# The causal mask of self-attention: added by VectorE in PSUM, or by a matmul on TensorE

## The chip, the cores and the metric

One core of one Trainium2 chip runs the whole kernel. Time is in device microseconds from one launch; three runs of the kernel before gave 2084.55, 2084.80 and 2087.17 us, and their median, 2084.8 us, is the time before. Beside these stands one execution under the profiler, to which every line of a profile here belongs.

## The reference

A decoder layer on x of shape (4, 512, 512): self-attention with a causal mask (16 query heads in 4 groups, each group with one key and value head, head size 128), cross-attention, and a mixture of 8 experts with a shared one, each behind a layernorm. The part that the change touches:

```python
scale = 1.0 / jnp.sqrt(jnp.float32(D))
scores = jnp.einsum('bsgqd,btgd->bgqst', q, k) * scale
causal = jnp.tril(jnp.ones((s, s), dtype=bool))
scores = jnp.where(causal, scores, jnp.finfo(scores.dtype).min)
attn = jax.nn.softmax(scores, axis=-1)
out = jnp.einsum('bgqst,btgd->bsgqd', attn, v)
```

Each of the 512 queries of a sequence sees the keys up to its own place.

## The kernel before

Self-attention is the first stage, some 900 us of the whole. It loops over 4 sequences (b), 4 groups (g) and 4 query heads of a group (h), that is 64 heads. Matrices are in float32, and TensorE does a float32 matmul in two passes, so that the profile shows two instructions for each.

For one head:

- `project` (L232) makes the transposed queries qT, 128 x 512, from four matmuls of 512 columns into a PSUM tile pq, which ScalarE copies and scales (L248). Once a group it makes the keys kT in the same way.
- `softmax_rows` (L251) goes over the four blocks of 128 queries (i). Block i sees (i + 1) * 128 keys. One matmul (L258) writes the scores to the PSUM tile sc, of which there are two buffers. Only the last 128 columns, the diagonal block, need a mask: a second matmul (L265) adds it in PSUM, with the identity `ident16` as weights and `mask16` (0 on and below the diagonal, -3.0e38 above) as data, both in bfloat16. VectorE then takes the negated maximum of each row from PSUM (`nmx`, L268), and ScalarE computes the exponentials into pr, with nmx as bias and the sums as a second output (L271). When the four blocks are done, VectorE takes the reciprocals of the sums (L279) and scales pr (L282).
- `attend` (L285) transposes pr in blocks of 128 x 128 on TensorE (L290: 1, 2, 3 and 4 transposes for the four blocks, ten in all, into the PSUM tile tp), has them copied to prT (L294: by ScalarE for block 1, by VectorE for the others), and multiplies with the values (L297) into po, which ScalarE copies (L305).
- After the fourth head of a group, `add_projection` (L308) multiplies with the output weights into pj and adds to x on VectorE (L319). The last sequence's is left for the next stage.

The program text calls `attend` of a head after `softmax_rows` of the next one (`late`, from L332). Within this stage the order on each engine isn't that of the text: a planner of the framework orders the instructions by its own estimate of when each one's inputs and buffers are ready. So one finds, on TensorE, transposes of the head before and projections of the next head between the score matmuls. Dependencies, and the waits for them, the framework finds by itself. [...]

`make_causal_mask` writes the float32 mask `maskf`; two casts on VectorE (L61, L65) make `ident16` and `mask16` at the start. In the stages behind, the order is for the most part pinned to that of the text, and they don't use the mask.

Of the kernel before, what the change touches and what calls it, by code (L numbers as in the profile page):

```python
# [9 lines left out]
BF16 = mybir.dt.bfloat16  # L10
AF = mybir.ActivationFunctionType
ALU = mybir.AluOpType
# [3 lines left out]
P = 128  # L16
# [19 lines left out]
def decoder_kernel(  # L36
# [15 lines left out]
    nc = tc.nc  # L52
    const = ctx.enter_context(tc.tile_pool(name="const", bufs=1))
# [3 lines left out]

    ident = const.tile([P, P], F32, tag="ident", name="ident")
    make_identity(nc, ident)
    ident16 = const.tile([P, P], BF16, tag="ident16", name="ident16")  # L60
    nc.vector.tensor_copy(ident16, ident)  # L61
    maskf = const.tile([P, P], F32, tag="maskf", name="maskf")
    make_causal_mask(nc, maskf, mask_val=MASK)
    mask16 = const.tile([P, P], BF16, tag="mask16", name="mask16")
    nc.vector.tensor_copy(mask16, maskf)  # L65
    ones16 = const.tile([P, P], BF16, tag="ones16", name="ones16")
    nc.gpsimd.memset(ones16, 1.0)

# [110 lines left out]
    with ExitStack() as ph:  # L179
# [71 lines left out]
        def softmax_rows(b, g, h, qT, kT):  # L251
            pr = p2.tile([P, 10 * P], F32, tag="pr", name=f"pr{b}_{g}_{h}")
            nmx = small.tile([P, NT], F32, tag="nmx", name=f"nmx{b}_{g}_{h}")
            sm = small.tile([P, NT], F32, tag="sm", name=f"sm{b}_{g}_{h}")
            for i in range(NT):
                n = (i + 1) * P
                sc = ps.tile([P, S], F32, tag="sc", name=f"sc{b}_{g}_{h}_{i}")
                nc.tensor.matmul(  # L258
                    sc[:, :n],
                    lhsT=qT[:, i * P : n],  # L260
                    rhs=kT[:, :n],
                    start=True,
                    stop=False,
                )
                nc.tensor.matmul(  # L265
                    sc[:, i * P : n], lhsT=ident16, rhs=mask16, start=False, stop=True
                )
                nc.vector.tensor_reduce(  # L268
                    nmx[:, i : i + 1], sc[:, :n], AX.X, ALU.max, negate=True
                )  # L270
                nc.scalar.activation(  # L271
                    pr[:, OFF[i] : OFF[i] + n],
                    sc[:, :n],
                    AF.Exp,
                    bias=nmx[:, i : i + 1],
                    accum_out=sm[:, i : i + 1],
                )
            rs = small.tile([P, NT], F32, tag="rs", name=f"rs{b}_{g}_{h}")
            nc.vector.reciprocal(rs, sm)  # L279
            for i in range(NT):  # L280
                q = pr[:, OFF[i] : OFF[i] + (i + 1) * P]
                nc.vector.tensor_scalar(q, q, rs[:, i : i + 1], None, ALU.mult)  # L282
            return pr
# [48 lines left out]
        for b in range(B):  # L332
            xnT, v = norm_and_v(b)
            for g in range(NKV):
                kT = project(b, g, QPG, xnT)
                outs = []
                for h in range(QPG):
                    qT = project(b, g, h, xnT)
                    pr = softmax_rows(b, g, h, qT, kT)
                    if late is not None:  # L340
                        finish(*late)
                    late = (b, g, h, pr, v, outs)
# [137 lines left out]
    with ExitStack() as ph:  # L480
# [329 lines left out]
        for i in range(NU * 8 + LAG + 4):  # L810
            n, step = divmod(i, 8)
# [92 lines left out]
    with ExitStack() as ph:  # L904
# [8 lines left out]
        for d in range(1, TT):  # L913
            nc.tensor.matmul(
                pos[:, d:, :],
                lhsT=ones16,
                rhs=sel[:, : TT - d, :],
                start=False,
                stop=d == TT - 1,
            )  # L920
        tot = ps.tile([P, E], F32, tag="tot", name="tot")
        for d in range(TT):
            nc.tensor.matmul(
                tot, lhsT=ones16, rhs=sel[:, d, :], start=d == 0, stop=d == TT - 1
# [56 lines left out]
        for op, value in ((ALU.bitwise_and, P - 1), (ALU.arith_shift_right, 7)):  # L981
            i = p2.tile([P, TT2], I32, tag=f"i{value}", name=f"i{value}")
# [7 lines left out]
        for k in range(2):  # L990
# [37 lines left out]
            for d in range(TT):  # L1028
                nc.tensor.matmul(
                    pick,  # L1030
                    lhsT=at_place[:, d],
                    rhs=nums[:, d],
                    start=k == 0 and d == 0,
                    stop=k == 1 and d == TT - 1,
# [165 lines left out]
```

## Time and profile before

| what | value |
|---|---|
| time before, median of three runs | 2084.8 us |
| the profiled execution | 2085.54 us |
| its span, first to last instruction | 2083.8 us |
| mean granted clock of TensorE | 0.997 |
| self-attention's score matmuls, first to last | 37.3 to 898.9 us |
| TensorE busy, 235 to 450 us | 214.0 of 215 us |
| VectorE busy, 235 to 450 us | 80.9 of 215 us |
| ScalarE busy, 235 to 450 us | 59.6 of 215 us |
| one head without a group's extra work | 9.375 us |

A line of the page's first part gives, for each engine, its busy time, the share of the span and the number of instructions. A line of the groups of instructions gives the line of the kernel, the engine, the operation, the tile written and the tiles read, the shape of the operands, how often, then the total busy time and the mean time of one (ns), then how long the engine stood idle before such instructions and for whom. A line of the timeline gives the start, the duration, the engine, the line and the operation; x2 or x4 are so many like instructions in a row, taken together, and a bracket at the end gives the idle time before it and what ended it. A matmul's duration holds the latency until its result is written, so the durations of successive matmuls overlap: what each takes from TensorE is read from start to start. PEld is the loading of the weights, which runs beside the matmuls.

### The profile page before, as it was taken

Reading aid. Unit: us, or ns where it says so; the run is one execution under the profiler, and the core shown is the slowest. Engines: PE = TensorE matmul, PEld = TensorE weight load, DVE = VectorE, ACT = ScalarE, POOL = GpSimd, SP = SyncE. Lnnn points to the kernel's source line nnn. Section 1 sums busy time; section 2 is a strip of 40 time slices with the busy share of each in tenths; the row PEclk is TensorE's granted clock in tenths of the full one; section 3 lists DMA queues with packets and bytes.
Section 4 is the critical chain, followed back from the end, with each engine's and each line's share of the span. In section 5 each row is a group of like instructions: output and inputs, shape, how many; then the busy total and the mean of one; then the engine's idle time right before and its main releaser. Section 6 shows DMA issues by size and latency. Waiting matters only on the chain. (4 is left out here: it accounts for less than half of the span.)

```text
span 2083.8 us, 22685 instructions
## 1 busy us (share of the span) xinstructions
PE 2029.6 (97%) x8507; PEld 948.5 (46%) x8507; DVE 864.6 (41%) x1843; ACT 679.5 (33%) x1479; POOL 197.3 (9%) x182
## 2 busy tenths in 40 slices
PE   7999999999999999999999999999999999999996
PEld 4555555554555555542233333333333445555553
DVE  4433344442344334436666656566563351111111
ACT  2322332232223323323555454444444101111121
POOL 1000000000000000010202202020200011222222
PEclk9999999999999999999999999999999999999999
DMA  7000000000000000010003100100110255323321
GB/s 282 0 1 0 1 0 1 0 0 1 0 1 0 1 0 0 1 32 14 16 16 100 32 16 22 42 15 13 42 27 1 95 199 160 59 56 57 57 49 23
DMA packets 52509, 74.81 MB, mean 36 GB/s; under 512 B 9889, under 2 KB 27809, under 8 KB 52402
## 3 DMA queue, kind: packets, MB, share of 16 engines
q1 hardware_dynamic: 43666, 54.73, 8.5%
q0 software_dynamic: 8736, 18.62, 4.7%
q8 instruction: 70, 1.15, 0.2%
q14 instruction: 37, 0.30, 0.0%
HBM read 47.60 MB, written 18.61 MB: 32 GB/s over the span
## 5 line engine op out<-in xcount | busy, mean ns | idle before, releaser
L362 DVE TENSOR_REDUCE cnmx<-s 128x1 f32<-128x512 f32 x512 | 329.3, 685 | 199.3 <-PE s L362 199.2
L362 ACT ACTIVATE w<-s 128x512 f32<-128x512 f32 x512 | 277.9, 595 | 339.0 <-PE s L362 338.9
L362 PE MATMUL s<-ckT,cqT 32*128 32x512 f32 x1024 | 308.8, 640 | 1.0 <-DVE cnmx L362 1.0
L236 PE MATMUL pq<-xnT,wqk 128*128 128x512 f32 x640 | 300.9, 593 | 0.0
L362 PE MATMUL s<-cqT,ckT 32*128 32x512 f32 x1024 | 294.8, 640 | 0.0
L268 DVE TENSOR_REDUCE nmx<-sc 128x1 f32<-128x128 f32 (+3 forms) x256 | 125.8, 491 | 185.0 <-PE sc L265 184.8
L271 ACT ACTIVATE pr<-sc,nmx 128x128 f32<-128x128 f32 (+3 forms) x256 | 135.0, 527 | 156.0 <-DVE nmx L268 156.0
L294 DVE COPY prT<-tp 128x128 f32<-128x128 f32 (+2 forms) x192 | 97.0, 507 | 206.4 <-PE tp L290 206.3
L258 PE MATMUL sc<-kT,qT 128*128 128x128 f32 (+3 forms) x512 | 181.4, 463 | 0.0
L312 PE MATMUL pj<-wpr,oT 128*128 128x512 f32 x384 | 171.8, 596 | 0.0
L362 PE MATMUL sh<-fnT,sw 128*128 128x512 f32 x320 | 154.0, 613 | 0.0
L297 PE MATMUL po<-prT,v 128*128 128x512 f32 (+3 forms) x512 | 149.5, 434 | 4.3 <-DVE prT L294 4.3
L236 PEld LDWEIGHTS pq<-xnT,wqk 128*128 128x128 f32 x640 | 110.7, 191 | 85.5 <-issue 85.4
L362 PEld LDWEIGHTS s<-cqT,ckT 32*128 32x128 f32 x1024 | 80.7, 183 | 145.3 <-ACT w L362 108.6
L1112 DVE TENSOR_TENSOR hm<-h,sl 128x352 f32<-128x352 f32 x39 | 20.5, 525 | 284.6 <-PE h L1102 279.1
L362 PE MATMUL cpo<-w,vpad 128*32 128x512 f32 x1024 | 137.3, 608 | 0.0
L297 PEld LDWEIGHTS po<-prT,v 128*128 128x128 f32 x512 | 96.8, 190 | 84.3 <-issue 45.4
L1124 PE MATMUL y<-w3all,hT 128*128 (+1 forms) x234 | 109.8, 605 | 15.1 <-DVE hT L1120 15.1
L248 ACT ACTIVATE qT<-pq 128x512 f32<-128x512 f32 x64 | 38.2, 597 | 225.0 <-PE pq L236 225.0
L258 PEld LDWEIGHTS sc<-kT,qT 128*128 128x128 f32 x512 | 81.6, 189 | 56.1 <-ACT qT L248 20.2
L312 PEld LDWEIGHTS pj<-wpr,oT 128*128 128x128 f32 x384 | 69.5, 190 | 77.3 <-issue 71.0
L290 PE MATMUL tp<-ident,pr 128*128 128x128 f32 x640 | 102.3, 275 | 1.3 <-DVE prT L294 1.3
(162 smaller groups left out, 2000.6 us busy)
## 6 DMA issues: line engine op xcount, KB each, us to landing
w1all<-in_w1T SPq DMA_DIRECT2D x8, 704.0 KB
w2all<-in_w2T SPq DMA_DIRECT2D x8, 704.0 KB
wqk<-in_wqkvT SPq DMA_DIRECT2D x4, 1280.0 KB
x<-in_x SPq DMA_DIRECT2D x4, 1024.0 KB
wpr<-in_wprojT SPq DMA_DIRECT2D x4, 1024.0 KB
cqT<-cxnT SPq DMA_DIRECT2D x128, 32.0 KB
ckT<-ctxT SPq DMA_DIRECT2D x128, 32.0 KB
normed<-fxn SPq DMA_DIRECT2D x4, 1024.0 KB
```

The source lines that it names most:

```text
L236: nc.tensor.matmul(pq, lhsT=wqk[g][:, c, h * D : (h + 1) * D], rhs=xnT[:, c, :], start=c == 0, stop=c == NC - 1,)
L248: nc.scalar.mul(t, pq, QSCALE)
L258: nc.tensor.matmul(sc[:, :n], lhsT=qT[:, i * P : n], rhs=kT[:, :n], start=True, stop=False,)
L268: nc.vector.tensor_reduce(nmx[:, i : i + 1], sc[:, :n], AX.X, ALU.max, negate=True)
L271: nc.scalar.activation(pr[:, OFF[i] : OFF[i] + n], sc[:, :n], AF.Exp, bias=nmx[:, i : i + 1], accum_out=sm[:, i : i + 1],)
L290: nc.tensor.transpose(t[:, j, :], pr[:, OFF[i] + j * P : OFF[i] + (j + 1) * P], ident)
L294: copy(prT[:, : i + 1, i * P : (i + 1) * P], t[:, : i + 1, :])
L297: nc.tensor.matmul(po[:, j * P :], lhsT=v[j][:, g, :], rhs=prT[:, j, j * P :], start=j == 0, stop=j == NT - 1,)
L312: nc.tensor.matmul(pj, lhsT=outs[h][:, s * P : (s + 1) * P], rhs=wpr[g][:, h, :], start=h == 0, stop=h == QPG - 1,)
L362: i = getattr(self.engine, name)(*args, **kw)
L1112: nc.vector.tensor_tensor(hm, h2, sl, ALU.mult)
L1124: nc.tensor.matmul(y, lhsT=hT[:m, ic, :], rhs=w3all[:m, e, ic, :], start=ic == 0, stop=ic == len(IC) - 1,)
```

## The change

The second matmul goes. The diagonal block of sc is instead read from PSUM by VectorE, added to `maskf` and written back to the same place, ahead of the reduction. The two casts and the tiles `ident16` and `mask16` go as well. Nothing else is changed.

```diff
     ident = const.tile([P, P], F32, tag="ident", name="ident")
     make_identity(nc, ident)
-    ident16 = const.tile([P, P], BF16, tag="ident16", name="ident16")
-    nc.vector.tensor_copy(ident16, ident)
     maskf = const.tile([P, P], F32, tag="maskf", name="maskf")
     make_causal_mask(nc, maskf, mask_val=MASK)
-    mask16 = const.tile([P, P], BF16, tag="mask16", name="mask16")
-    nc.vector.tensor_copy(mask16, maskf)
...
                     lhsT=qT[:, i * P : n],
                     rhs=kT[:, :n],
                     start=True,
-                    stop=False,
-                )
-                nc.tensor.matmul(
-                    sc[:, i * P : n], lhsT=ident16, rhs=mask16, start=False, stop=True
+                    stop=True,
+                )
+                nc.vector.tensor_tensor(
+                    sc[:, i * P : n], sc[:, i * P : n], maskf, ALU.add
                 )
                 nc.vector.tensor_reduce(
                     nmx[:, i : i + 1], sc[:, :n], AX.X, ALU.max, negate=True
```

So in every block the reduction, and behind it the exponentials and the release of the buffer of sc, follow an instruction of VectorE instead of one of TensorE.

## The prediction

> **What bounds the kernel now.** I read the page first, then the groups of instructions by shape in the attention stage, then the timeline of one head on TensorE, VectorE and ScalarE, then the waits.
>
> ```profile
> PE 2029.6 (97%) x8507; PEld 948.5 (46%) x8507; DVE 864.6 (41%) x1843; ACT 679.5 (33%) x1479; POOL 197.3 (9%) x182
> ```
>
> TensorE sets the time, and VectorE is under half busy. From the groups by shape, two rows (busy us and mean ns after the bar):
>
> ```profile
> L265 PE MATMUL sc<-mask,ident 128*128 128x128 bf16 x256 | 56.1, 219 | 0.0
> ...
> L319 DVE TENSOR_TENSOR x<-pj,x 128x512 f32<-128x512 f32 x48 | 33.2, 691 | 111.5 <-PE pj L312 111.5
> ```
>
> The mask matmul's 219 ns is latency, not what it takes from TensorE. For that, read start to start on the TensorE timeline of one head, which recurs every 9.375 us (start, duration; x2 are the two passes of one float32 matmul, and the second start is not shown):
>
> ```profile
> 408.88 0.39 PE L258 MATMUL sc<-kT,qT 128*128 128x128 f32 x2
> 409.10 0.22 PE L265 MATMUL sc<-mask,ident 128*128 128x128 bf16 x1
> 409.16 0.65 PE L258 MATMUL sc<-kT,qT 128*128 128x256 f32 x2
> 409.64 0.22 PE L265 MATMUL sc<-mask,ident 128*128 128x128 bf16 x1
> 409.70 0.61 PE L290 MATMUL tp<-ident,pr 128*128 128x128 f32 x4
> 410.19 0.91 PE L258 MATMUL sc<-kT,qT 128*128 128x384 f32 x2
> 410.94 0.22 PE L265 MATMUL sc<-mask,ident 128*128 128x128 bf16 x1
> 411.00 1.10 PE L258 MATMUL sc<-kT,qT 128*128 128x512 f32 x2
> ```
>
> From 409.10 to 409.16: a mask costs TensorE 0.055 us. The transposes between row blocks 1 and 2 belong to the head before; they are cover. The chain through the other engines, first VectorE and then ScalarE:
>
> ```profile
> 404.36 0.18 DVE L279 RECIPROCAL rs<-sm 128x4 f32<-128x4 f32 x1 [0.25 <-ACT pr L271]
> 404.57 1.27 DVE L282 TENSOR_SCALAR pr<-pr,rs 128x128 f32<-128x128 f32 x4
> ...
> 409.36 0.29 DVE L268 TENSOR_REDUCE nmx<-sc 128x1 f32<-128x128 f32 x1 [1.06 <-PE sc L265]
> 409.90 0.43 DVE L268 TENSOR_REDUCE nmx<-sc 128x1 f32<-128x256 f32 x1 [0.25 <-PE sc L265]
> ```
>
> ```profile
> 409.68 0.37 ACT L271 ACTIVATE pr<-sc,nmx 128x128 f32<-128x128 f32 x1 [0.93 <-DVE nmx L268]
> ```
>
> The tile sc has two buffers, so row block 2's matmul needs the exponential of block 0, and block 3's that of block 1. Exponential 0 ends at 410.05, and the matmul starts 0.14 later, at 410.19. So TensorE already waits on this chain. The waits say it for block 3 (us in total, times, the longest), 0.25 us a head:
>
> ```profile
> PEld sc L258 <- ACT pr L271: 16.0, 63, 0.3
> ```
>
> The idle time of TensorE in a head: 0.06 behind mask 0 (the stream of a mask is too short to hide the next weight load); 0.16 at block 2 (the four transposes take 0.44, so they end at 410.14, and block 2, weights first, streams from 410.30, since its own 0.64 of streaming ends at 410.94); 0.085 at block 3 (it streams for 0.855 before 411.94, where its mask starts; hence from 411.085, against 411.00). Together 0.305.
>
> **What the Trainium skill says.** "TensorE: Matmul & The Clock Gate", back-to-back issue gap, gives N/2.4 + 2.5 ns, 56 ns for 128 columns; the trace has 0.055 us. "VectorE: DVE Perf Modes", the errata section, gives (N+151)/0.96 ns for a float32 tensor_tensor: 691 at 512, just what L319 shows, and 291 at 128. "Perfetto Trace Analysis", optimization strategy, says that a gap that repeats on the saturated engine "can mean there isn't enough SBUF/PSUM for the next tile"; the 0.25 us wait, 63 times, is that.
>
> **The change, part by part.** All sums are against the profiled execution, 2085.5 us (span 2083.8 and 1.7 around it); the median of the runs shown, 2084.8, is 0.7 lower.
>
> Removed, two casts at the start (0.20 and 0.22 us on VectorE): at most 0.2 us of the first layernorm. I take nothing: TensorE's first real matmuls, from 14.25, run beside weights that are still being loaded (the DMA engines are over 90% busy there), and these loads don't get earlier.
>
> Removed, 256 mask matmuls: 4 x 0.055 = 0.22 us a head, and the 0.06 idle behind mask 0. Blocks 0 and 1 are then through TensorE at 409.53 (two passes of 0.11 from 408.88, two of 0.213 from 409.10), 0.17 before 409.70.
>
> Added, 256 adds on VectorE, PSUM and SBUF in, PSUM out. No instruction of before writes PSUM from VectorE. The nearest row is L319 by the formula above, 0.29 us; the bounds are 0.27 and 0.35. The reduction reads what the add wrote: a dependent pair starts 0.03 after the first one's end (404.36 + 0.18, then 404.57). VectorE has the time: 4 x 0.29 on some 4.6 busy in 9.375.
>
> What this moves in the chain, first with TensorE's order as it is. Matmul 0's second pass starts at 408.99, lasts 0.28, and VectorE follows 0.04 later (as from the mask's end, 409.32, to 409.36): add 0 at 409.31 to 409.60, reduction 0 from 409.63 instead of 409.36. Everything behind it is 0.27 late: exponential 0 ends at 410.32, and block 2 streams from 410.57. Add 1 is queued behind reduction 0 (consecutive VectorE instructions overlap by 0.08): 409.84 to 410.13; reduction 1 to 410.58; exponential 1 from 410.61 to 411.08; block 3 may load at 411.22 and streams from 411.335, for 0.86, to 412.195. In the profile its mask is done at 412.00. So a head becomes 0.195 longer, although 0.22 of matmuls went. Behind that there is cover: adds 2 and 3 delay the copies to prT to some 414.0, where po was to start at 414.05; the scaling of L282 has 1.8 us of slack before its transposes.
>
> But TensorE's order is a planner's. It has put transposes of the head before, and projections, where the scores aren't ready: four transposes as shown, but in the first heads it was three and a projection:
>
> ```profile
> 52.69 0.50 PE L290 MATMUL tp<-ident,pr 128*128 128x128 f32 x3
> 53.02 1.02 PE L236 MATMUL pq<-xnT,wqk 128*128 128x512 f32 x2
> 53.88 0.81 PE L258 MATMUL sc<-kT,qT 128*128 128x384 f32 x2
> ```
>
> There block 2 doesn't wait (0.81 for its two passes, against 0.91). With a chain that is longer by 0.27 and two masks fewer ahead of the cover, 0.17 earlier, a planner that sees the add has about 0.4 more to fill: four more transposes at 0.11, but only three are left (three of a head's ten are done earlier, four are there). I take all seven. Each moved ahead of block 2 saves 0.11 behind block 3: 0.195 - 3 x 0.11 = -0.135 a head. Times 63 heads that have such cover: -8.5 us. The last head has nothing to cover it: its later add and copies cost some 0.45. Sum: -8, so 2077.5 profiled, or 2076.8 as a median.
>
> **The rivals**, as medians, the last head's 0.45 in each. *Full cover* (faster): the planner puts a projection (0.86 us) ahead of block 2, as in the early heads. All idle time goes with the masks: 0.22 + 0.305 = 0.525 a head, 33 us, 2052. For it: that the pattern exists; against: that the planner left it by the fourth head. A projection between blocks 2 and 3 alone lies between: with seven transposes, block 2 ends at 411.21, the projection at 412.07, block 3 at 412.93, against 413.19 before for the same work: -0.26, -16 us, 2069. I count it to the forecast's case.
>
> *Balance*: six transposes (-0.025 a head), or seven with an add of 0.35, which comes in twice in block 3's chain (-0.135 + 0.12): within 2 us of 2084.
>
> *The wait grows* (slower): four or five transposes stay ahead of block 2, because the planner prices the add below its real latency. The place is block 2's and 3's wait for the exponentials; the price 0.195 a head, 12 us, 2097 at four (0.315, 20 us, with an add of 0.35); it decides below six transposes, 0.195/0.11 = 1.8 above four. For it: that today's order already leaves 0.16 and 0.085 idle, so the planner is late by that much.
>
> *A worse order* (slower): the adds, waiting at the head of VectorE's queue for their matmul, hold back the copies to prT and with them po. Over 2100. Against it: 1.8 us of slack, and a VectorE half idle.
>
> **How the numbers follow.** Forecast 0.33; full cover 0.22; balance 0.10; the wait grows 0.25; a worse order 0.10. Change within 0.2% (4 us) is about what a measurement here can't tell from none. Faster 0.55, same 0.10, slower 0.35. The likeliest case's own range, from a projection ahead of block 3 to an add of 0.35, is 2069 to 2084. The range of 8 in 10 reaches from full cover to the growing wait with some of the dearer add: 2051 to 2100; it leaves out the worse order and the ends of the two neighbours.
>
> **What would show it.** On the timeline of a head: the number of transposes between blocks 1 and 2 (seven), block 2's start against exponential 0's end (0.14), the period (9.24; 9.57 if the wait grows, 8.85 with full cover). An add of 0.29 us and a reduction 0.03 behind it. The wait of block 3 for the exponential still there. Wrong if the add isn't within 0.27 to 0.35, if the order of TensorE is unchanged, or if another wait than the exponentials' ends last.

## The result, and the profile after

| | time before | time after | ratio, 95% interval |
|---|---|---|---|
| median of four runs each | 2085.94 us | 2070.34 us (2068.06 to 2070.88) | 0.9923 (0.9906 to 0.9941) |
| span of the profiled execution | 2083.8 us | 2066.2 us | |

The change makes the kernel 15.6 us faster, less than 1%. The forecast was 8. (The median before is of one run more than the 2084.8 us above.) In the changed kernel L254 is the score matmul, L261 the add, L264 the reduction, L267 the exponential, L286 the transposes, L293 po, L232 the projections. First the page's line of busy times, then the add's row among the groups of instructions (busy us and mean ns after the bar):

```profile
PE 2012.8 (97%) x8251; PEld 940.1 (45%) x8251; DVE 923.2 (45%) x2097; ACT 679.8 (33%) x1479; POOL 197.1 (10%) x182
...
L261 DVE TENSOR_TENSOR sc<-sc,maskf 128x128 f32<-128x128 f32 x256 | 75.3, 294 | 157.7 <-PE sc L254 157.7
```

TensorE has 256 instructions fewer and is still busy for 97% of the span, so it remains the bound. VectorE has 58.6 us more to do than its 864.6 before and is still under half busy: as a load the adds are no matter, only as links of a chain. The add takes 294 ns.

Next, one head of the changed kernel on TensorE's timeline:

```profile
105.20 0.82 PE L254 MATMUL sc<-kT,qT 128*128 128x128 f32 x4
105.85 0.93 PE L286 MATMUL tp<-ident,pr 128*128 128x128 f32 x7
106.79 0.91 PE L254 MATMUL sc<-kT,qT 128*128 128x384 f32 x2
107.54 1.02 PE L232 MATMUL pq<-xnT,wqk 128*128 128x512 f32 x2
108.40 1.02 PE L254 MATMUL sc<-kT,qT 128*128 128x512 f32 x2
109.26 2.32 PE L293 MATMUL po<-prT,v 128*128 128x512 f32 x8
...
114.32 0.82 PE L254 MATMUL sc<-kT,qT 128*128 128x128 f32 x4
```

Three things are new besides the missing masks. Seven transposes, not four, stand between blocks 1 and 2. A projection stands between blocks 2 and 3. And po follows block 3 at once, since no transposes are left to be done there. From 105.20 to 114.32 the head takes 9.12 us, where it was 9.375.

The chain through VectorE and ScalarE in the same head:

```profile
105.62 0.30 DVE L261 TENSOR_TENSOR sc<-sc,maskf 128x128 f32<-128x128 f32 x1 [1.01 <-PE sc L254]
105.96 0.29 DVE L264 TENSOR_REDUCE nmx<-sc 128x1 f32<-128x128 f32 x1
106.17 0.29 DVE L261 TENSOR_TENSOR sc<-sc,maskf 128x128 f32<-128x128 f32 x1
106.28 0.37 ACT L267 ACTIVATE pr<-sc,nmx 128x128 f32<-128x128 f32 x1 [1.21 <-DVE nmx L264]
106.38 0.56 DVE L290 COPY prT<-tp 128x384 f32<-128x384 f32 x1
106.55 0.19 ACT L267 ACTIVATION_READ_ACCUMULATOR pr<-sc,nmx 128x1 f32 x1
106.79 0.30 PEld L254 LDWEIGHTS sc<-kT,qT 128*128 128x128 f32 x2 [0.25 <-ACT pr L267]
106.86 0.41 DVE L264 TENSOR_REDUCE nmx<-sc 128x1 f32<-128x256 f32 x1
```

The reduction starts 0.04 after the add's end (105.62 + 0.30, then 105.96), exponential 0 ends at 106.65, and block 2's weights are loaded 0.14 later. The chain has one link more than the prediction named: ScalarE reads out the row sums, the second output of the exponential, with an instruction of its own, which ends at 106.74. In the trace the semaphore that the weight load waits for is raised by this read and not by the exponential, in all 256 blocks, and the load starts 0.05 after its end. So 0.09 of the 0.14 us is the read of the sums; no run here leaves it out. Where the text below says that a matmul waits for an exponential, this read is the last part of it.

Block 2 streams until 107.54 and takes 0.64, so it starts to stream at 106.90. The transposes were through at 106.62 (0.11 each from 105.85). So 0.28 us of idle is left, all of it at block 2, where it had been 0.16. Block 3 doesn't hold up TensorE any more: 0.86 from 108.40 to 109.26 is just its streaming. A copy to prT now stands ahead of reduction 1, so exponential 1 is later still, and the projection covers that too. The waits of the score matmuls' weight loads for the exponentials (us in total, times, the longest):

```profile
PEld sc L254 <- ACT pr L267: 32.7, 120, 0.8
```

They are now two a head. (Before, only block 3's was listed, 63 times; block 2's left PEld idle for just 0.12.) The one at block 3 is a weight load that waits under the projection, and costs nothing.

Where the 17.6 us of the span come from can be read from the start of each head's first score matmul in both traces. The first one came 0.7 earlier. Over the next four heads, which the planner ordered differently, 1.2 more was gained. From there on each of 56 steps from head to head is shorter by 0.25 (14.2 us) and each of the three at the starts of sequences 1, 2 and 3 by 1.0 (3.1 us). Together 19.1 us at the last head (896.15 to 877.02). About 1.5 us of it is lost again by the end of the span, which is less than the runs of the changed kernel differ among themselves (2.8 us).

The starts of sequences gain more because of the next sequence's layernorm. Before, its transposes (L171) ran into a wait in the last head of each sequence:

```profile
229.58 0.60 PE L171 MATMUL t<-ident,xn 128*128 128x128 f32 x4
230.85 0.44 PE L171 MATMUL t<-ident,xn 128*128 128x128 f32 x2 [0.68 <-ACT xnT L172]
```

In the changed kernel four of these transposes stand between blocks 2 and 3, as a projection does elsewhere, and the wait is gone:

```profile
223.15 0.91 PE L254 MATMUL sc<-kT,qT 128*128 128x384 f32 x2
223.90 0.60 PE L167 MATMUL t<-ident,xn 128*128 128x128 f32 x4
224.33 1.04 PE L254 MATMUL sc<-kT,qT 128*128 128x512 f32 x2
...
227.36 1.04 PE L167 MATMUL t<-ident,xn 128*128 128x128 f32 x8
```

### The profile page after: what moved, and what is told of

The parts are those of the page before. It is cut to its first block, busy times and chain, and to the rows that moved or that the text cites. A ratio compares the mean times of both kernels' runs of the same rounds, so it can differ in the third digit from the quotient of the medians.

```text
span 2066.2 us, 22429 instructions
## 1 busy us (share of the span) xinstructions
PE 2012.8 (97%) x8251; PEld 940.1 (45%) x8251; DVE 923.2 (45%) x2097; ACT 679.8 (33%) x1479; POOL 197.1 (10%) x182
## 5 line engine op out<-in xcount | busy, mean ns | idle before, releaser
L232 PE MATMUL pq<-xnT,wqk 128*128 128x512 f32 x640 | 301.0, 593 | 0.0
L267 ACT ACTIVATE pr<-sc,nmx 128x128 f32<-128x128 f32 (+3 forms) x256 | 134.9, 527 | 230.2 <-DVE nmx L264 230.1
L254 PE MATMUL sc<-kT,qT 128*128 128x128 f32 (+3 forms) x512 | 176.7, 447 | 1.1 <-ACT pr L267 0.2
L232 PEld LDWEIGHTS pq<-xnT,wqk 128*128 128x128 f32 x640 | 114.1, 190 | 96.6 <-issue 84.6
L293 PE MATMUL po<-prT,v 128*128 128x512 f32 (+3 forms) x512 | 149.3, 434 | 3.2 <-DVE prT L290 3.2
L261 DVE TENSOR_TENSOR sc<-sc,maskf 128x128 f32<-128x128 f32 x256 | 75.3, 294 | 157.7 <-PE sc L254 157.7
L293 PEld LDWEIGHTS po<-prT,v 128*128 128x128 f32 x512 | 96.9, 190 | 85.1 <-issue 46.8
L264 DVE TENSOR_REDUCE nmx<-sc 128x1 f32<-128x128 f32 (+3 forms) x256 | 125.0, 488 | 6.4
L254 PEld LDWEIGHTS sc<-kT,qT 128*128 128x128 f32 x512 | 81.2, 189 | 77.1 <-ACT pr L267 32.7
```

The costliest lines, as they stand in the source:

```text
L232: nc.tensor.matmul(pq, lhsT=wqk[g][:, c, h * D : (h + 1) * D], rhs=xnT[:, c, :], start=c == 0, stop=c == NC - 1,)
L254: nc.tensor.matmul(sc[:, :n], lhsT=qT[:, i * P : n], rhs=kT[:, :n], start=True, stop=True,)
L261: nc.vector.tensor_tensor(sc[:, i * P : n], sc[:, i * P : n], maskf, ALU.add)
L264: nc.vector.tensor_reduce(nmx[:, i : i + 1], sc[:, :n], AX.X, ALU.max, negate=True)
L267: nc.scalar.activation(pr[:, OFF[i] : OFF[i] + n], sc[:, :n], AF.Exp, bias=nmx[:, i : i + 1], accum_out=sm[:, i : i + 1],)
L293: nc.tensor.matmul(po[:, j * P :], lhsT=v[j][:, g, :], rhs=prT[:, j, j * P :], start=j == 0, stop=j == NT - 1,)
```

## The experiments

The change does two things at once: it exchanges an instruction, and it lets the planner find another order. My theory was that the order makes the gain, by covering a chain that the add makes longer, and that the add under the old order would be a loss. The rival was that taking the mask off TensorE is itself the gain. To set one without the other, the order has to be fixed. So the loops of the self-attention stage were replaced by a list of operations, in the order in which the trace and the program of a kernel have them on TensorE, VectorE and ScalarE. Everything behind this stage is as it was.

```diff
+ORDER = """... sc0110 add0110 red0110 exp0110 sc0111 add0111
+tp01020 tp01021 tp01022 cp0102 red0111 exp0111 tp01030 ..."""
...
+                    i = getattr(self.engine, name)(*args, **kw)
+                    tc.keep_in_program_order(i)
...
+        for word in ORDER.split():
+            kind = word.rstrip("0123456789")
+            do(kind, tuple(int(d) for d in word[len(kind) :]))
```

The digits are sequence, group, head and block; sc is a score matmul, mk the mask by a matmul, add the mask by VectorE, red the reduction, exp the exponential, tp a transpose and cp its copy to prT, pq and pj projections. In the profiles of these kernels every operation of the stage has one line, that of the loop. What each came to, with the period of a plain head read from its trace as before (the kernel before was run again beside each group of these runs, with medians from 2084.8 to 2086.0 us, and the ratios are to those runs; a difference of 1 or 2 us is within what runs of one kernel differ by):

| order of the stage | mask | us | ratio to before, 95% interval | head, us |
|---|---|---|---|---|
| before | matmul | 2085.74 | 0.9999 (0.9990 to 1.0008) | 9.375 |
| before | add | 2098.37 | 1.0060 (1.0043 to 1.0077) | 9.58 |
| before | none | 2070.82 | 0.9925 (0.9908 to 0.9941) | 9.15 |
| before, three buffers of sc | add | 2056.07 | 0.9857 (0.9841 to 0.9874) | 8.87 |
| after | matmul | 2078.46 | 0.9962 (0.9948 to 0.9976) | 9.24 |
| after | add | 2070.48 | 0.9919 (0.9902 to 0.9935) | 9.12 |
| after, projection behind block 3 | add | 2077.64 | 0.9961 (0.9947 to 0.9975) | 9.25 |
| after | two adds | 2093.26 | 1.0036 (1.0023 to 1.0048) | 9.45 |
| after | none | 2052.45 | 0.9847 (0.9831 to 0.9864) | 8.85 |
| full cover | matmul | 2076.91 | 0.9959 (0.9945 to 0.9973) | 9.24 |
| full cover | add | 2054.27 | 0.9848 (0.9832 to 0.9865) | 8.85 |

**The orders written out, with nothing changed.** Each kernel's own order, with its own way of masking.

> The order of the kernel before on TensorE, VectorE and ScalarE, written out, with the mask by the matmul: the written-out order is to be no change of its own. If the order of the instructions is all that the planner contributes: the same as the kernel before within 0.2% (2081 to 2090 us), period of a head 9.375 us. If the writing-out costs something of its own, the experiments with a written-out order are to be read against this run and not against the kernel before.

> The order of the changed kernel written out, with VectorE's add. If the order is all: as the changed kernel, 0.992 (2068 to 2073 us), period 9.12 us. Otherwise the difference is the price of the writing-out.

Both came out as the planned kernels, in time and in the head's period. So the order of the instructions accounts for what the planner contributes, as far as these times can tell, and the others may be compared with the kernel before and the changed one.

**The add in the old order.** Against the written-out order of before:

```diff
-            elif k == "mk":
-                pe.matmul(
-                    T[("sc", *a)][:, n - P : n], lhsT=ident16, rhs=mask16, start=False, stop=True
-                )
+            elif k == "add":
+                dve.tensor_tensor(d, d, maskf, ALU.add)
```

> Every instruction of self-attention stands in the order of the kernel before on each engine, written out and pinned; only the mask is VectorE's add, right ahead of its reduction. Theory A (TensorE's order is what decides): the add lengthens the chain that ends at blocks 2 and 3 and nothing new covers it, +0.195 us a head over some 60 heads, so about 12 us slower than before, ratio 1.006, period of a head 9.57 us. Theory B (the gain is the masks' own TensorE time, 4 x 0.055 + 0.06 a head): the gain is there in the old order too, ratio 0.992, period near 9.1.

It came out as the theory has it: 2098.37 us. In this order the exchange by itself makes the kernel slower by 13.6 us. TensorE's timeline, and ScalarE's exponential 0:

```profile
404.36 0.82 PE L448 MATMUL sc<-kT,qT 128*128 128x128 f32 x4
405.02 0.60 PE L448 MATMUL tp<-ident,pr 128*128 128x128 f32 x4
...
405.44 0.37 ACT L448 ACTIVATE pr<-sc,nmx 128x128 f32<-128x128 f32 x1 [1.21 <-DVE nmx L448]
...
405.95 1.90 PE L448 MATMUL sc<-kT,qT 128*128 128x384 f32 x4 [0.34 <-ACT pr L448]
```

Four transposes end at some 405.46. Exponential 0 ends at 405.81, and block 2 starts 0.14 later, as above. Counted to where block 2 streams, 0.11 behind that, TensorE is idle for 0.60 us, where it was 0.16 before. Of the 0.44 more, 0.28 comes from the longer chain (from the head's first score matmul to the end of exponential 0 it is 1.45 us, and was 1.17), and 0.16 from the cover, which ends earlier because the two masks are gone.

**The new order with the matmul.** The opposite edit, on the written-out order of after.

> Every instruction of self-attention stands in the order of the changed kernel, pinned; but the mask is the matmul again, right behind its score matmul, and the adds are gone. Theory A: blocks 2 and 3 no longer wait, since seven transposes and a projection cover the shorter chain, and the masks take 0.28 a head, which is what the changed kernel idles at block 2: period 9.12, ratio to before 0.992, the same as the changed kernel. Theory B: the masks' time comes back, ratio 1.000.

The order alone brings 6 to 8 us (6 by the medians, 8 by the ratio), not the 16 that I expected. Block 2 waits for nothing, as expected, but the masks cost more than their stream:

```profile
404.08 0.22 PE L451 MATMUL sc<-mask,ident 128*128 128x128 bf16 x1
404.14 0.65 PE L451 MATMUL sc<-kT,qT 128*128 128x256 f32 x2
404.63 0.22 PE L451 MATMUL sc<-mask,ident 128*128 128x128 bf16 x1
404.68 0.94 PE L451 MATMUL tp<-ident,pr 128*128 128x128 f32 x7
405.45 0.81 PE L451 MATMUL sc<-kT,qT 128*128 128x384 f32 x2
406.10 0.22 PE L451 MATMUL sc<-mask,ident 128*128 128x128 bf16 x1
406.16 1.08 PE L451 MATMUL pq<-xnT,wqk 128*128 128x512 f32 x2
407.07 1.02 PE L451 MATMUL sc<-kT,qT 128*128 128x512 f32 x2
```

The projection pq takes 0.91 from 406.16 to 407.07; without a mask ahead of it, it takes 0.86 (107.54 to 108.40 above). In the same way block 1 takes 0.49, which is two passes of 0.213 and 0.06 more. A mask streams for 0.055 us, and the likely reason for the gap is that the weights of the float32 matmul behind it can't be loaded in so short a time. In "TensorE: Matmul & The Clock Gate" of the Trainium skill, the section "LDWEIGHTS" gives P/1.2 ns for a weight load, 107 for 128 columns (the traces have 0.11 from the start of block 2's weights to its streaming), of which, as an estimate, a stream of 55 leaves 52 uncovered; the trace shows 0.05 to 0.06. No run changes the weight load alone, so this reason is not shown by itself. I had seen this 0.06 behind mask 0 of before and had not carried it over to the masks whose next matmul, in the new order, no longer waits for something else. The masks cost 4 x 0.055 and three times this gap, 0.385 us a head, and the periods say 9.24 - 8.85 = 0.39.

**No mask at all, in both orders.** These two kernels leave the causal mask out of self-attention (neither mk nor add is in the list), which leaves the time of everything else.

> The changed kernel's order, pinned, with no mask at all: neither add nor matmul, so self-attention sees every key of its blocks. Theory A (block 2's remaining wait is the add's latency in the chain): exponential 0 ends 0.33 earlier, before the seventh transpose is done, so nothing waits: period 8.84, about 16 us less than the changed kernel, ratio to before 0.985. Rival (block 2 waits for something else, such as the release of its buffer by ScalarE's accumulator read): ratio 0.992, no gain over the changed kernel.

> The order of the kernel before, pinned, with no mask at all (self-attention sees every key of its blocks). Theory A: block 2 still waits for exponential 0, 0.05 earlier than before, block 3 no longer, and the masks' streams are gone: 0.23 us a head less, some 60 heads, 14 us, ratio 0.993. So the waits keep most of the 0.525 a head (33 us) that masks and idle time took, although the masks are free. Rival (masks and idle time go together): ratio 0.984, as in the new order without a mask.

Both came out as expected. The old order saves 14 to 15 us with its masks gone, 0.22 us a head, which is their stream alone. Its idle time stays:

```profile
393.81 0.60 PE L430 MATMUL tp<-ident,pr 128*128 128x128 f32 x4
394.42 1.80 PE L430 MATMUL sc<-kT,qT 128*128 128x384 f32 x4
396.05 0.49 PE L430 MATMUL tp<-ident,pr 128*128 128x128 f32 x3
```

The four transposes end at 394.25, and block 2 streams from 394.53, 0.11 behind 394.42: 0.28 of idle. Blocks 2 and 3 stream for 0.64 and 0.86 of the 1.63 until 396.05, which leaves 0.02 for block 3. Together it is 0.30, as it was with the masks (0.305): what the masks and the idle time behind mask 0 leave free, block 2's wait takes.

The new order with no mask is at 8.85 us a head. So in the new order the add costs 17.9 us (2070.34 - 2052.45) and the matmul 26.0; in the old one the add costs 27.6 and the matmul 14 to 15. Which of the two is cheaper depends on the order around them.

**Two adds in the new order.** The second adds a tile of zeros.

```diff
-                dve.tensor_tensor(d, d, maskf, ALU.add)
+                for m in (maskf, zero):
+                    dve.tensor_tensor(d, d, m, ALU.add)
```

> The changed kernel's order, pinned, with a second add, of zeros, behind each add: 0.29 + 0.04 us more in the chain from matmul 0 to block 2. Theory A (block 2's wait takes the add's latency in full, block 3 has a projection as cover): period 9.12 + 0.33 = 9.45, 18 to 20 us more than the changed kernel, 2089, ratio 1.002. Rival (the adds lie beside other work): ratio 0.992, no change to the changed kernel; or, if block 3 counts too, another 0.33 a head, ratio 1.011.

It is 22.9 us slower than the changed kernel, somewhat more than expected. A head is longer by 0.33 us, which is one add of 0.29 and one step of 0.04 to the instruction behind it. What is added to this chain comes out at the end one for one:

```profile
403.07 0.91 PE L450 MATMUL sc<-kT,qT 128*128 128x384 f32 x2 [0.34 <-ACT pr L450]
403.82 1.02 PE L450 MATMUL pq<-xnT,wqk 128*128 128x512 f32 x2
404.68 1.02 PE L450 MATMUL sc<-kT,qT 128*128 128x512 f32 x2
405.54 2.32 PE L450 MATMUL po<-prT,v 128*128 128x512 f32 x8
```

Only block 2 waits; block 3's 0.86 until 405.54 is its streaming. The second add ahead of reduction 1 and the copies around it are covered by the projection ahead of block 3.

**Full cover.** In 53 heads, the projection that stood between blocks 2 and 3 is moved ahead of block 2.

```diff
-tp01031 tp01032 tp01033 cp0103 sc0112 add0112 red0112 exp0112 pq0121 sc0113
+tp01031 tp01032 tp01033 cp0103 pq0121 sc0112 add0112 red0112 exp0112 sc0113
```

> The changed kernel's order, pinned, with one move in the 53 heads that have the pattern: the projection between blocks 2 and 3 stands ahead of block 2. Theory A (what is left idle, 0.28 us a head, is block 2's wait for the longer chain with the add): the projection covers it, period 8.84, 53 x 0.28 = 15 us less than the changed kernel, 2055, ratio to before 0.985. Rival: block 3 then waits in its place (its exponential ends at the same time as before), or po waits for the copies to prT: no gain over the changed kernel, ratio 0.992.

2054.27 us: it beats the kernel before by 30 us and the changed one by 16.

```profile
407.21 0.93 PE L449 MATMUL tp<-ident,pr 128*128 128x128 f32 x7
407.97 1.02 PE L449 MATMUL pj<-wpr,oT 128*128 128x512 f32 x2
408.83 1.67 PE L449 MATMUL sc<-kT,qT 128*128 128x384 f32 x4
410.34 2.32 PE L449 MATMUL po<-prT,v 128*128 128x512 f32 x8
```

Blocks 2 and 3 take 1.51 us together (408.83 to 410.34), with no idle time before or between. The head is at 8.85, as with no mask: under this cover the add is free. The planner had this place for the projection and put it one matmul later; its order leaves 0.28 us a head unused.

> The full-cover order with the mask matmul instead of the add. A mask takes 0.055 us of stream, and 0.055 more where a float32 weight load follows: in this order all four masks of a head are followed by one, 4 x 0.11 = 0.44 us a head, 28 us over 64 heads: 2054.3 + 28 = 2082 us (0.998). If a mask costs its stream alone, 0.22 us a head: 2068 us (0.992). Either way the add beats the matmul under full cover.

In the same order the matmul costs 22.6 us, between the two figures. Of the four masks three are followed by a matmul that shows the gap, not four: behind mask 1 come the transposes, and their seven take 0.77, as against 0.76 without a mask. The head is at 9.24, as in the new order with the matmul. Without a wait for the exponentials, the place of the projection makes no difference.

**The projection behind block 3.** The opposite of full cover, to test the step of the prediction that had left block 3 right behind block 2. Reduction 1 is put ahead of the copies, as the prediction had it.

```diff
-sc0111 add0111 tp01020 tp01021 tp01022 cp0102 red0111 exp0111
+sc0111 add0111 red0111 exp0111 tp01020 tp01021 tp01022 cp0102
...
-sc0112 add0112 red0112 exp0112 pq0121 sc0113 add0113 red0113 exp0113 po0100
+sc0112 add0112 red0112 exp0112 sc0113 add0113 red0113 exp0113 pq0121 po0100
```

> The new order with the add, but in 53 heads the projection between blocks 2 and 3 stands behind block 3 instead, and reduction 1 directly behind add 1: the order that the sum of the prediction assumed. If the projection's place is what made the difference between the forecast's 8 us and the measured 15.6: block 3 waits some 0.13 us for exponential 1, block 2 still 0.28 us, a head takes 9.25 us, and the kernel 2070.3 + 53 x 0.13 = 2077 us (0.996). If block 3's wait was gone for another reason: as the changed kernel, 9.12 us a head and 2070 us.

2077.64 us and 9.25 a head: in these heads this is the order that the prediction had summed, at 9.24.

```profile
404.90 0.93 PE L448 MATMUL tp<-ident,pr 128*128 128x128 f32 x7
...
405.84 1.90 PE L448 MATMUL sc<-kT,qT 128*128 128x384 f32 x4
...
407.57 1.02 PE L448 MATMUL pq<-xnT,wqk 128*128 128x512 f32 x2
```

From 405.84 to 407.57 it is 1.73. Streaming takes 0.64 and 0.86, loading block 2's first weights 0.11; the other 0.12 is block 3's wait for exponential 1.

**A third buffer of sc.** The old order with the add, where it lost 13.6 us, with three buffers for sc and one for po in place of two and two (the stage keeps eight PSUM buffers in all).

```diff
+        PBUFS = {'t': 2, 'mm': 2, 'sc': 3, 'po': 1}
...
+                key, lambda: ps.tile(list(shape), F32, tag=tag, name=name, bufs=PBUFS[tag])
```

> As the old order with the add (2098), pinned, but with three PSUM buffers for sc and one for po, instead of two each. Theory A (the wait is for a free buffer of sc): block 2 starts at once, block 3 needs only exponential 0: period 8.87, 0.7 a head less than the old order with two buffers, 2054, ratio 0.985. Rival (the chain binds elsewhere, at po, which waits for the copies to prT that stand behind the reductions on VectorE): po takes over, ratio 0.995 to 1.003.

2056.07, as expected: 42 us less than with two buffers. Block 2 follows the four transposes at once, and block 3 follows block 2:

```profile
397.07 0.60 PE L448 MATMUL tp<-ident,pr 128*128 128x128 f32 x4
...
397.51 1.67 PE L448 MATMUL sc<-kT,qT 128*128 128x384 f32 x4
```

So the chain through VectorE, which is as long as before, costs time only through the buffer that it holds.

**A third buffer, with the planner free.** The changed kernel with `bufs=3` on the tile sc and `bufs=1` on po.

> The changed kernel with the planner free, and only the buffers changed: three for sc, one for po. Theory A: with a third buffer no order has to hide the chain, so the planner's own order comes out near full cover: 2052 to 2057, ratio 0.985. Rival (one buffer of po, or the planner's new order, makes another wait): no better than the changed kernel, ratio 0.992 or more.

2067.59 us, a ratio of 0.9908 (0.9891 to 0.9924), hardly to be told from the changed kernel. This is a miss. With the third buffer the planner runs blocks 0, 1 and 2 in a row and leaves two transposes ahead of block 3:

```profile
400.58 1.46 PE L254 MATMUL sc<-kT,qT 128*128 128x128 f32 x6
...
401.88 0.38 PE L286 MATMUL tp<-ident,pr 128*128 128x128 f32 x2
...
402.18 1.12 PE L254 MATMUL sc<-kT,qT 128*128 128x512 f32 x2
```

```profile
401.66 0.37 ACT L267 ACTIVATE pr<-sc,nmx 128x128 f32<-128x128 f32 x1 [1.21 <-DVE nmx L264]
```

Block 3 is now the one that takes over the buffer of block 0. Exponential 0 ends at 402.03, block 3's weights come 0.15 later, and its 0.96 until 403.14 holds 0.10 of idle; 0.08 more lies ahead of it (two transposes take 0.22 of the 0.30). The wait went along with the order, 0.18 us a head in place of 0.28. Besides, po's weight loads now wait for copies to prT more often than in the changed kernel, where it was 5.5 us in 7 waits:

```profile
PEld po L293 <- DVE prT L290: 20.6, 26, 1.2
```

I haven't separated how much of that is on TensorE's time.

## Why the prediction was right, and where its size was off

- **What bounds the kernel, and the chain.** Right. TensorE stays the bound, and the wait of block 2 for exponential 0 ends last. It can be removed by cover (8.85) or by a buffer (8.87).
- **Removed, the masks.** The sum took out 4 x 0.055 and the 0.06 behind mask 0. In the old order without a mask 0.22 a head came back, and the 0.06 went into block 2's wait. But 0.055 isn't what a mask costs in an order without waits; there it is 0.39 a head. I had quoted the skill's formula for the gap, 56 ns. The same section of that page, "Back-to-back issue gap", warns that at small N it counts too little, for want of the weight loads. The trace agrees that it is more, with 0.11 us for a mask and its gap; the page has 81 ns at 128 columns.
- **Removed, the casts, at nothing.** Nothing speaks against it: the first score matmul came 0.7 earlier, but in the written-out orders it came at 36.33 with the casts (order before, matmul) and at 37.21 without them (order before, add), so it differs from kernel to kernel by about as much.
- **Added, the add of 0.29, a reduction 0.03 behind it.** 0.294 and 0.04. The 291 ns by the formula of the Trainium skill's "VectorE: DVE Perf Modes", errata section, hold within 1% here, where an input and the result are in PSUM.
- **Block 2, 0.14 behind exponential 0.** The number is right; 0.09 of it is the read of the sums, which the prediction didn't name. It lies in both kernels alike.
- **The chain 0.27 late, a head 0.195 longer in the old order.** Measured 0.205 (9.58), and 2098.37 us where the rival of the growing wait had 2097.
- **All seven transposes ahead of block 2.** Right, in every plain head.
- **What stands between blocks 2 and 3.** This is the term that was mis-sized. "Each moved ahead of block 2 saves 0.11 behind block 3" left block 3 right behind block 2, waiting for exponential 1, and made -0.135 a head. The planner put a projection there. For that variant I had written -0.26, and 0.255 was measured; I counted it to the forecast's case but didn't sum with it. The difference, 0.125 us in 63 heads, is 7.9 us, about as much as the forecast was short of 15.6. With the projection put behind block 3, a head takes 9.25, where the forecast had 9.24. That the whole kernel then comes so near the forecast's 2076.8 is in part luck. In its profiled execution the steps from head to head bring 7.4 us, where the forecast had 8.5; the starts of the sequences bring 3.1 and the first four heads 1.2 that it didn't have; and this execution is 2.5 us shorter than the median. The order could have been suspected: once the transposes are used up, a planner has only projections to fill the gap that is left.
- **63 heads with such cover, and 0.45 for the last one.** 56 steps of 0.25; three ends of sequences with 1.0, where the wait of the layernorm's transposes went, which I had not looked at; the first heads differ. From the last head's first score matmul to the first matmul of the next stage it was 0.14 longer, not 0.45.
- **The rivals.** Full cover is real, at 8.85 us a head as worked out and 2054 us instead of 2052, but the planner didn't choose it. It didn't come to the growing wait either, because it did move the transposes; with them left in place the wait grew as priced. Why it prefers the later place for the projection wasn't tried.

## What to carry to other kernels

A short matmul on the bound engine costs its stream and the gap behind it (here 0.055 us each); both come back only where no wait takes their place. Moving such work to an engine that is half idle lengthens a chain, and whether this costs anything was decided here by the number of buffers and by what stood ahead of the instruction that takes over the buffer: the same add cost 27.6 us, 17.9 us or next to nothing. When a planner orders the work, a change is first of all a new order: write the order down, fix it, and change one thing at a time, and then try moving one independent piece of work ahead of the wait that is left.

## What the hardware showed that I had not expected

- The gap behind a bfloat16 matmul of 128 columns shows ahead of block 1, of a projection, of block 3 and of po (0.05 to 0.06 us each), but not ahead of a row of seven transposes (0.77 against 0.76 us). In the same trace (new order, matmul) a weight load takes 0.14 us for a transpose and 0.19 for a float32 matmul, which would fit; no run tests it.
- A third PSUM buffer for the scores, in the old order, and a projection moved by one place, in the new one, end at nearly the same: 8.87 and 8.85 us a head, though neither shortens the chain.
- The release of a PSUM buffer by an exponential that also gives its row sums comes with the read of the sums: it ends 0.09 us behind the exponential, and the weight load that waits for the buffer starts 0.05 behind it.
